# Routing as a chain of its own beside the next group's attention, for the first four groups

## The chip, the cores and the metric

The kernel runs on one core of a Trainium2 chip. The metric is the device time of one execution in microseconds; the time of a kernel is the median of its runs. The engines are TensorE (PE, with its weight loads as PEld), VectorE (DVE), ScalarE (ACT), GpSimd (POOL) and SyncE (SP, which only issues transfers here). Each takes its own instructions in order and waits on semaphores for what others make; POOL and SP also issue DMAs.

## The reference

One decoder layer over 64 sequences of 128 tokens with 256 features, all in f32: a selective-scan (Mamba) block, a retention-style attention over a context, and a mixture of experts, each followed by a layernorm of the sum with its input.

```
x = layernorm(x + mamba(x))          # layernorm, W_in, conv of 4 taps, silu, scan, gate, W_out, + x
x = layernorm(x + retention(x, ctx)) # q from x, k and v from ctx, rotated; scores * decay; @ v
x = layernorm(x + ffn(x))

# ffn, for each token t:
shared   = (silu(x Wg) * (x Wu)) Wd
probs    = sigmoid(x @ router.T + bias)          # 8 experts
w        = the two largest probs over their sum
combined = sum over the two experts e of w[t,e] * ((silu(x Wg_e) * (x Wu_e)) Wd_e)
ffn      = shared + combined
```

## The kernel before

The 64 sequences are worked off in 16 groups of four (512 tokens, `T`). A group passes through these steps, each a Python generator that issues instructions and yields:

- `front` and `scan` (together `first_half`): layernorm, W_in, convolution, gate, and the scan as products of masked matrices. They leave `acc`, in the buffer `sz`.
- `after`: W_out (`x1`, in a ring buffer of two that is also called x2), layernorm, `kh` and `v` from the context, `qh` from x1, scores, and the result `x2` with its layernorm.
- `route`: `turned` transposes x2 to `x2T`; the router's logits go through TensorE, ACT (exp) and VectorE, which ranks the experts and counts how many tokens of each expert lie before (`count`, kept from group to group); then 8 indirect DMAs (L1028), four from the row buffer of x2 and four from `row1`, a second copy, scatter the tokens' rows into `xs` in HBM, ordered by expert. ACT makes the copy row1 (L1002); VectorE adds slot and weight (L1022, L1024).
- `early_shared`: the shared expert of the group, from x2T (`shared_hidden`, `shared_down`), and a store of the sum. For the groups in `LATE` (7 to 12) it is left for the end of the kernel.
- `tile_list(k)` and `refill`: when enough groups have been routed (4, 8, 12, 16, 16), a list of expert tiles is made on VectorE, and fetches of rows and weights are issued on SP.
- `one_tile`: a tile of 256 (later 128) rows through its expert: `rows_turned`, `hidden`, `down`; results are scattered to `ys`.

The order is not written out by hand. `abreast` runs several chains of such generators together. Each chain has a position, which `placed` moves from `at` to `at + span` as its work passes, and `abreast` always advances the chain with the lowest position that isn't pausing. A yielded number is a pause, in microseconds of the planned TensorE work counted in `work`. `until` holds a chain in place until a flag is set in `states`. The chains of the first stage are:

- `first_halves` (and `second_start` for group 1): first_half(g), placed from g - 1 to g
- `second_halves`: for each group `second_half`, that is `after`, a pause, `route` and, where due, `tile_list` and `refill`, placed from g + 1 to g + 2
- `shared_ones`: early_shared(g) when the group is routed and is not in LATE
- `tiles_beside`: 57 of the 78 tiles

So in one chain the attention of group g + 1 begins after the routing of group g has ended. The instructions issued in this order then go through a scheduler that fixes the order on each engine and puts in the waits. A later instruction may be moved ahead of one that isn't ready by the scheduler's own reckoning; on the chip an engine never passes an instruction by.

Buffers carry waits too. In the pool `one` each tag has one buffer, and `qh` (of `after`) and `row1` (of `route`) share the tag "qh": a qh or a row1 can only be written when the scatters out of the last row1 have landed and the last qh has been read. `pm` has five PSUM banks, for nearly everything outside the experts, `gu` three, for gate and up products. `mhalf` and `pow` on POOL are part of every layernorm (`rstd`, L588), and so every layernorm passes through the queue in which the scatters stand.

After the first stage (`second_halves` and the rest have ended) a second `abreast` does the other 21 tiles, and a third the late shared experts and the final sums.

Of the kernel before, what the change touches and what calls it, by code (L numbers as in the profile page):

```python
# [41 lines left out]
NT = sum(n for _, _, n, _ in BATCHES)  # L42
DX = D + 2
MOST = max(n for _, _, n, _ in BATCHES)
LATE = range(7, 13)


# [455 lines left out]
def shared_decay(K):  # L503

    with ExitStack() as ctx:
        _shared_decay(ctx, K)


def _shared_decay(ctx, K):
# [114 lines left out]
    def load_x(g):  # L627
        xt = xts[g % 3]
        nc.gpsimd.dma_start(out=xt, in_=x[g * GB : (g + 1) * GB].rearrange("b l d -> l b d"))
        return xt  # L630
# [315 lines left out]
    def route(g, st):  # L946
# [79 lines left out]
        for k in range(2):  # L1026
# [6 lines left out]
            yield 5.0  # L1033
        if g in LATE:
            nc.sync.dma_start(out=x2_rows[g].rearrange("p (b d) -> p b d", d=D), in_=x2)
# [33 lines left out]
    def early_shared(g, st):  # L1069
        hid = yield from shared_hidden(st["x2T"], ring, 4)  # L1070
        yield 1.7
        for _ in shared_down(st["x2"], hid, st["x2"], gu):
            yield
        nc.sync.dma_start(out=x2_rows[g].rearrange("p (b d) -> p b d", d=D), in_=st["x2"])
# [21 lines left out]
    def tile_list(k):  # L1096
# [41 lines left out]
        nc.vector.tensor_tensor(skip[:, 0 : NE - 1], d[0:1, 1:NE], skip[:, 0 : NE - 1], ALU.add)  # L1138
        ge = small.tile([1, MOST, NE], F32, name="ge", bufs=1)[:, 0:n, :]
        nc.vector.tensor_tensor(  # L1140
# [6 lines left out]
        nc.vector.tensor_tensor(ge, ge, skip.unsqueeze(1).to_broadcast([1, n, NE]), ALU.mult)  # L1147
        row = small.tile([1, MOST], F32, name="row", bufs=1)[:, 0:n]
        nc.vector.tensor_reduce(row, ge, AX.X, ALU.add)
# [30 lines left out]
    def refill():  # L1180

        for part in range(2):
            while fetched[part] < min(room[part], known[0]):
                (fetch_down if part else fetch)(fetched[part])
                fetched[part] += 1
# [98 lines left out]
    def one_tile():  # L1284

        i = listed[0]
        listed[0] += 1
        refill()
        yield max(0.0, there[i] - work[0])
        made = yield from hidden(i)  # L1290
        room[0] = i + 1 + NW
        refill()
        if waiting:
            yield from down(*waiting.pop())
        waiting.append((i, *made))
        room[1] = i + NW
        refill()
        yield
# [13 lines left out]
    def abreast(*chains):  # L1312

        alive = [[gen, whole, 0.0, 0.0] for gen, whole in chains]
        while any(c[1] for c in alive):
            able = [c for c in alive if c[3] <= work[0]]
            if not able:
                work[0] = min(c[3] for c in alive)  # L1320
                continue
            c = min(able, key=lambda c: c[2])
            try:
                c[2], wait = next(c[0])
            except StopIteration:
                alive.remove(c)
                continue
            c[3] = work[0] + wait

    def placed(gen, at, length, span=1.0):  # L1330

        passed = 0.0
        while True:
            before = work[0]
            try:
                wait = next(gen) or 0.0
            except StopIteration:
                return
            passed += work[0] - before + wait
            yield at + span * min(1.0, passed / length), wait  # L1340

    def first_half(st):
        yield from front(st)
        yield from scan(st)

    def second_half(g, st):
        yield from after(g, st)
        yield 2.6
        yield from route(g, st)
        for k, (groups, *_) in enumerate(BATCHES):  # L1350
            if groups == g + 1:
                tile_list(k)
                refill()


    states = [{} for _ in range(NG)]
# [139 lines left out]
    def until(ready, at):  # L1496
        while not ready():
            yield at, 0.5

    def first_halves():  # L1500
        states[2]["xt"] = load_x(2)
        yield from placed(start, 0.0, 54.0)
        states[0]["scanned"] = True
        for g in range(2, NG):
            if g + 1 < NG:
                yield from until(lambda: "read" in states[g - 2], g - 1)
                states[g + 1]["xt"] = load_x(g + 1)
            yield from placed(first_half(states[g]), g - 1, 54.0)
            states[g]["scanned"] = True

    def second_start():
        yield from placed(first_half(states[1]), 0.2, 54.0)
        states[1]["scanned"] = True

    def second_halves():
        for g in range(NG):
            yield from until(lambda: "scanned" in states[g] and (g < 2 or "added" in states[g - 2]), g + 1)
            yield from placed(second_half(g, states[g]), g + 1, 60.0)
            states[g]["routed"] = True
            if g in LATE:  # L1520
                states[g]["added"] = True

    def shared_ones():

        for g in range(NG - 1):
            if g not in LATE:
                at, length = (g + 2.55, 0.45) if g + 2 in [groups for groups, *_ in BATCHES[1:]] else (g + 2, 1.0)
                yield from until(lambda: "routed" in states[g], at)
                yield from placed(early_shared(g, states[g]), at, 23.0, length)
                states[g]["added"] = True  # L1530

    def tiles_beside():

        for at, length in places:
            if at >= NG + 1:
                return
            i = listed[0]
            while i == known[0]:
                yield at, 1.0
            yield from placed(one_tile(), at, 11.0, length)  # L1540

    abreast((first_halves(), True), (second_start(), True), (second_halves(), True), (shared_ones(), True), (tiles_beside(), True))
    chains.close()


# [2 lines left out]
    def late_shared(g, last):  # L1548


        if not loaded:
            load_late(g)
            yield 4.0
        x2, x2T = loaded.pop()
        if not last:
            load_late(g + 1)
        made = shared_hidden(x2T, late, 6)
        for c in range(CF):
            yield next(made)
            if c == 1:  # L1560
                y = load_products(g)
                if unsummed:
                    yield from summed(*unsummed.pop())
        try:
            next(made)
        except StopIteration as end:
            hid = end.value
        unsummed.append((g, x2, y, hid))
        if last:
            yield 1.7  # L1570
            yield from summed(*unsummed.pop())
# [33 lines left out]
    )  # L1605
    early = [g for g in range(NG) if g not in LATE]

# [4 lines left out]
    def all_shared():  # L1612
        for i, g in enumerate(LATE):
            yield from placed(late_shared(g, g == LATE[-1]), i / len(LATE), 25.0, 1 / len(LATE))

# [221 lines left out]
```

## Time and profile before

| what | us |
|---|---|
| time, median of 3 runs | 1934.27 (1934.08 to 1934.54) |
| profiled execution, its own time | 1935.52 |
| its span in the trace | 1933.7 |
| TensorE busy | 1866.0 (97%) |
| VectorE busy | 971.9 (50%) |
| ScalarE busy | 748.7 (39%) |
| GpSimd busy | 473.1 (24%) |
| mean granted TensorE clock | 0.988 |

A matrix product in f32 shows in the trace as two matmuls and two weight loads. Matmul ends are modelled, so that the busy time of TensorE holds overlaps of neighbours; an idle time before an instruction is given in square brackets in a timeline, with what ended it. A view of busy time by stretches gives for each engine the busy time and, in brackets, the instructions; the clock is the mean of the granted TensorE clock over the stretch. A view of waits lists: engine, tile and line, what it waited for, then the time in all, how often, and the longest. Line numbers are those of the kernel before.

The first routing's logits go through TensorE at 124 us, and the scatters of the four groups' routings begin at 148.4, 214.6, 287.1 and 359.9 us.

### The profile page before, as it was taken

Reading aid. Unit: us, or ns where it says so; the run is one execution under the profiler, and the core shown is the slowest. Engines: PE = TensorE matmul, PEld = TensorE weight load, DVE = VectorE, ACT = ScalarE, POOL = GpSimd, SP = SyncE. Lnnn points to the kernel's source line nnn. Section 1 sums busy time; section 2 is a strip of 40 time slices with the busy share of each in tenths; the row PEclk is TensorE's granted clock in tenths of the full one; section 3 lists DMA queues with packets and bytes.
Section 4 is the critical chain, followed back from the end, with each engine's and each line's share of the span. In section 5 each row is a group of like instructions: output and inputs, shape, how many; then the busy total and the mean of one; then the engine's idle time right before and its main releaser. Section 6 shows DMA issues by size and latency. Waiting matters only on the chain.

```text
span 1933.7 us, 26599 instructions
## 1 busy us (share of the span) xinstructions
PE 1866.0 (97%) x9252; PEld 1393.1 (72%) x9252; DVE 971.9 (50%) x2409; ACT 748.7 (39%) x1238; POOL 473.1 (24%) x715
## 2 busy tenths in 40 slices
PE   7799999999999998999999999999999999999997
PEld 3656656668686856787877768786877888999554
DVE  5766667745455557455555474554333111111774
ACT  5553553443434343535353544352231222222233
POOL 2102212303030403132322313141313322222111
PEclk9999999999999998999999999999999999999998
DMA  4211211423150214323242224232204443353782
GB/s 142 53 35 44 68 49 41 137 85 95 45 153 28 85 35 153 101 77 113 64 133 93 79 93 123 61 123 92 81 19 128 146 150 118 120 175 107 276 305 89
DMA packets 101352, 199.10 MB, mean 103 GB/s; under 512 B 22904, under 2 KB 61432, under 8 KB 96600
## 3 DMA queue, kind: packets, MB, share of 16 engines
q1 hardware_dynamic: 80952, 144.24, 23.6%
q0 software_dynamic: 17328, 51.41, 7.8%
q10 hardware_dynamic: 2928, 1.65, 0.3%
q8 instruction: 75, 1.23, 0.3%
q14 instruction: 69, 0.57, 0.1%
HBM read 206.81 MB, written 58.08 MB: 137 GB/s over the span
## 4 chain that ended last, share of the span: by engine, by line
PE 72%; DVE 3%; issue 3%; DMA 2%; ACT 2%; POOL 2%; SPq 0%; POOLq 0%; ACTq 0%; DVEq 0%
PE pm L545 37%; PE gu L545 32%; PE pm L549 4%; DMA picked<-ys 1%; POOL rstd L588 1%; DMA ys<-rows_out,to 1%; DVE st L583 0%; DVE x L1305 0%; DMA cq<-chunks 0%; POOL xs L1028 0%; ACT x L593 0%; ACT xn L593 0%; DVE hc L1051 0%; DVE xt L1305 0%; ACT xc L667 0%
## 5 line engine op out<-in xcount | busy, mean ns | idle before, releaser
L545 PE MATMUL gu<-rows_T,routed_gu 128*128 128x256 f32 (+1 forms) x2496 | 499.4, 351 | 1.5 <-ACT rows_T L1232 1.5
L545 PEld LDWEIGHTS gu<-rows_T,routed_gu 128*128 128x128 f32 x2496 | 417.7, 191 | 59.2 <-issue 14.2
L1261 DVE TENSOR_TENSOR hid<-hid,gu 128x512 f32<-128x512 f32 x135 | 92.7, 687 | 394.8 <-PE gu L545 344.4
L545 PE MATMUL pm<-routed_d,hid 128*128 128x256 f32 x1080 | 252.7, 381 | 0.0
L545 PE MATMUL gu<-x2T,shared_w 128*128 128x512 f32 x512 | 232.0, 596 | 4.4 <-DVE hc L1051 3.3
L545 PE MATMUL pm<-xnT,w_in_s 128*128 128x512 f32 x480 | 226.6, 599 | 1.7 <-ACT xnT L606 1.1
L545 PEld LDWEIGHTS pm<-routed_d,hid 128*128 128x128 f32 x1080 | 199.7, 190 | 29.6 <-issue 5.4
L1277 POOL DMA_INDIRECT ys<-rows_out,to x135 | 135.0, 1000 | 331.4 <-ACT rows_out L1276 282.8
L545 PEld LDWEIGHTS gu<-x2T,shared_w 128*128 128x128 f32 x512 | 94.3, 190 | 112.1 <-issue 93.6
L593 ACT ACTIVATE x<-x,shift,rstd 128x256 f32<-128x256 f32 x156 | 82.3, 590 | 232.5 <-DVE shift L590 222.2
L588 POOL TENSOR_TENSOR rstd<-var,mhalf 128x4 f32<-128x4 f32 (+1 forms) x69 | 72.8, 1055 | 370.6 <-DVE var L586 318.6
L662 DVE SCALAR_TENSOR_TENSOR xc<-pm,cw,xc 128x508 f32<-128x508 f32 (+1 forms) x180 | 131.4, 738 | 37.2 <-ACT xc L657 36.0
L545 PEld LDWEIGHTS pm<-xnT,w_in_s 128*128 128x128 f32 x480 | 90.2, 192 | 80.3 <-issue 72.3
L1276 ACT ACTIVATE rows_out<-pm,wt 128x256 f32<-128x256 f32 x135 | 57.9, 471 | 205.2 <-PE pm L545 185.4
L1260 ACT ACTIVATE hid<-gu 128x512 f32<-128x512 f32 x135 | 80.6, 597 | 110.0 <-PE gu L545 109.7
L545 PE MATMUL pm<-w_out_s,sz 128*128 128x256 f32 x512 | 116.4, 381 | 0.4 <-ACT xd L807 0.2
L545 PEld LDWEIGHTS pm<-w_out_s,sz 128*128 128x128 f32 x512 | 95.4, 191 | 14.3 <-issue 1.0
L657 ACT ACTIVATE xc<-pm,cb,cw 128x512 f32<-128x512 f32 x60 | 46.7, 778 | 144.2 <-PE pm L545 144.2
L1028 POOL DMA_INDIRECT xs<-x,index x64 | 71.6, 1118 | 78.0 <-DVE row L1024 42.8
L583 DVE BATCH_NORM_STATS2 st<-x 128x6 f32<-128x256 f32 x196 | 77.4, 408 | 1.6 <-DMA x<-in_x_dram 0.7
L545 PE MATMUL gu<-shared_w,hc 128*128 128x256 f32 x320 | 72.5, 380 | 0.0
L1051 DVE TENSOR_TENSOR hc<-hc,gu 128x512 f32<-128x512 f32 x64 | 43.5, 680 | 55.2 <-PE gu L545 35.1
(288 smaller groups left out, 2571.2 us busy)
## 6 DMA issues: line engine op xcount, KB each, us to landing
routed_gu<-in_ffn_dram SPq DMA_DIRECT2D x78, 1024.0 KB
routed_d<-in_ffn_dram SPq DMA_DIRECT2D x78, 512.0 KB
picked<-ys SPq DMA_DIRECT2D x16, 1024.0 KB
rows_in<-xs SPq DMA_DIRECT2D x57, 258.0 KB
cT<-in_ctxT_dram POOLq DMA_DIRECT2D x16, 512.0 KB, 4.1
x_rows<-x SPq DMA_DIRECT2D x16, 512.0 KB
cq<-chunks SPq DMA_DIRECT2D x15, 512.0 KB
x<-in_x_dram POOLq DMA_DIRECT2D x9, 512.0 KB, 4.2
```

The costliest lines, as they stand in the source:

```text
L545: nc.tensor.matmul(out, lhsT=lhsT, rhs=rhs, **how)
L549: nc.tensor.transpose(out, src, ident)
L583: nc.vector.bn_stats(st, src[:, b, :])
L588: nc.gpsimd.tensor_tensor(rstd, var, mhalf[:, 0:n], ALU.pow)
L593: nc.scalar.activation(dst[:, b, :], src[:, b, :], AF.Identity, bias=shift[:, b : b + 1], scale=rstd[:, b : b + 1])
L657: nc.scalar.activation(xcf[:, c, :], ps, AF.Identity, bias=cb[:, c : c + 1], scale=cw[:, c, TAPS - 1 : TAPS],)
L662: nc.vector.scalar_tensor_tensor(xc[:, c, :, s:], ps3[:, :, : L - s], cw[:, c, TAPS - 1 - s : TAPS - s], xc[:, c, :, s:], ALU.mult, ALU.add,)
L1028: s = nc.gpsimd.indirect_dma_start(out=xs, in_=rows[k][:, b, :], in_offset=None, out_offset=bass.IndirectOffsetOnAxis(ap=index[:, b, k : k ...
L1260: nc.scalar.activation(hc, psg, AF.Silu)
L1261: nc.vector.tensor_tensor(hc, hc, psu, ALU.mult)
L1276: nc.scalar.activation(y[:, j, :], ps[:, j, :], AF.Copy, scale=wt[:, j : j + 1])
L1277: s = nc.gpsimd.indirect_dma_start(out=ys, in_=y[:, j, :], in_offset=None, out_offset=bass.IndirectOffsetOnAxis(ap=to[:, j : j + 1], axis=0),)
```

## The change

For the groups 0 to 3 (`APART`) the chain `second_halves` now runs only `after`, placed from g + 1 to g + 1.6, and goes on to the attention of the next group. A new chain, `routings`, waits until x2 of the group is there, pauses 2.6 as the old chain did, and runs `routing` (the rest of the old second_half: `route`, `tile_list`, `refill`) placed from g + 1.6 to g + 2. Group 4 and later ones are issued as before; `second_halves` holds there until the group before is routed. The instructions are the same ones; what `abreast` issues, and the scheduler orders, is their interleaving.

```diff
+APART = range(0, 4)
 ...
     def second_half(g, st):
         yield from after(g, st)
         yield 2.6
+        yield from routing(g, st)
+
+    def routing(g, st):
         yield from route(g, st)
         for k, (groups, *_) in enumerate(BATCHES):
             if groups == g + 1:
                 tile_list(k)
                 refill()
 ...
     def second_halves():
         for g in range(NG):
             yield from until(lambda: "scanned" in states[g] and (g < 2 or "added" in states[g - 2]), g + 1)
+            if g in APART:
+                yield from placed(after(g, states[g]), g + 1, 38.0, 0.6)
+                continue
+            yield from until(lambda: g == 0 or "routed" in states[g - 1], g + 1)
             yield from placed(second_half(g, states[g]), g + 1, 60.0)
             states[g]["routed"] = True
             if g in LATE:
                 states[g]["added"] = True
+
+    def routings():
+
+        for g in APART:
+            yield from until(lambda: "x2" in states[g], g + 1.6)
+            yield g + 1.6, 2.6
+            yield from placed(routing(g, states[g]), g + 1.6, 26.0, 0.4)
+            states[g]["routed"] = True
 ...
-    abreast((first_halves(), True), (second_start(), True), (second_halves(), True), (shared_ones(), True), (tiles_beside(), True))
+    abreast((first_halves(), True), (second_start(), True), (second_halves(), True), (routings(), True), (shared_ones(), True), (tiles_beside(), True))
```

## The prediction

> **What bounds the kernel now.** I read the page's busy rows and slices first, then the busy time by stage, then TensorE's waits, then GpSimd's timeline.
>
> ```profile
> span 1933.7 us, 26599 instructions
> PE 1866.0 (97%) x9252; PEld 1393.1 (72%) x9252; DVE 971.9 (50%) x2409; ACT 748.7 (39%) x1238; POOL 473.1 (24%) x715
> PE   7799999999999998999999999999999999999997
> PEclk9999999999999998999999999999999999999998
> ```
>
> TensorE is the bound: the span less its busy time is 67.7 us, and the change removes no work. It can win only idle time and time at a reduced clock. Here a rule speaks for much more. The Trainium skill ("Perfetto Trace Analysis", section Identifying the Most-Contended Engine) says that matmul busy share is no measure of headroom and that the weight loads' busy share is: 72%, or 28% of 1933.7 = 540 us left. Those 540 us are no time that an order of chains can fill: 400 to 720 us shows loads 230.1 of 320 us and no idle matmul time at all. I use the waits; by the rule a gain of tens of microseconds would be within reach.
>
> ```profile
> core 0: us, PE busy (x) PEld busy (x) DVE busy (x) ACT busy (x) POOL busy (x), PEclk, DMA share, GB/s
> 93.00:145.00 52.00, 45.76 (x205) 25.79 (x204) 35.21 (x78) 27.27 (x41) 5.68 (x5) 0.93 0.12 33
> 145.00:218.00 73.00, 71.61 (x348) 47.37 (x347) 47.25 (x129) 35.27 (x54) 19.13 (x17) 0.98 0.18 55
> 218.00:290.00 72.00, 69.47 (x335) 44.89 (x335) 48.84 (x122) 34.14 (x53) 15.74 (x16) 1.00 0.18 53
> 290.00:355.00 65.00, 62.45 (x277) 40.33 (x276) 43.05 (x108) 29.43 (x47) 11.15 (x12) 1.00 0.15 47
> 355.00:400.00 45.00, 41.17 (x208) 28.15 (x207) 33.45 (x88) 17.82 (x28) 16.58 (x24) 0.96 0.54 191
> 400.00:720.00 320.00, 320.00 (x1553) 230.10 (x1553) 170.92 (x407) 130.57 (x210) 68.79 (x79) 1.00 0.23 70
> 720.00:748.00 28.00, 20.77 (x128) 18.02 (x125) 20.90 (x74) 9.45 (x14) 11.59 (x10) 0.76 0.31 99
> ```
>
> ```profile
> PE pm L549 <- ACT xn L593: 8.7, 9, 2.0
> PE pm L545 <- DVE sel L985: 2.8, 1, 2.8
> ```
>
> Each stretch: length, then busy time of each engine, then clock. From 93 us (where routing begins to matter) to 400, where group 3's routing has been turned into expert tiles, TensorE idles 6.2 + 1.4 + 2.5 + 2.6 + 3.8 = 16.5 us, and the clock costs at most 52 x 0.07 + 73 x 0.02 + 45 x 0.04 = 6.9 us. So the four routings that move lie in a region with only 23 us to win. The second view's two rows are its longest waits from 90 to 400 us (in all, times, longest): most are the transposes of a later group's normalized x, one is routing's own (sel). Another pocket is 720 to 748 us (7.2 us idle, 28 x 0.24 = 6.7 us of clock), when group 7's routing runs and the fillers have run out.
>
> ```profile
> 148.43 1.11 POOL L1028 DMA_INDIRECT xs<-x,index  x1 [14.29 <-ACT xd L807]
> 149.84 0.99 POOL L1028 DMA_INDIRECT xs<-x,index  x1 [0.30 <-DVE xc L817]
> 158.01 0.96 POOL L1028 DMA_INDIRECT xs<-row,index  x1 [0.30 <-issue]
> 378.77 0.19 POOL L1234 CAST to<-rows_in 128x2 int32<-128x2 f32 x1 [3.10 <-DMA rows_in<-xs]
> 379.04 1.05 POOL L588 TENSOR_TENSOR rstd<-var,mhalf 128x4 f32<-128x4 f32 x1
> ```
>
> A routing ends in eight scatters on GpSimd's queue: from 148.43 to 158.97 is 10.5 us, and the view of that line has 2.6 us (median) from issue to landing, so the eighth lands some 13 us after its row is written. The last two rows are a queue effect: a layernorm's rstd stands behind the first tile's `to`, which waits for fetched rows.
>
> **The change, part by part.** No instruction is added or removed but a few ACT table loads (929 against 917 in the program's order; 12 x 1.28 us on an engine 39% busy, hidden by its slack). What moves is the order on all engines, from TensorE's first changed row, after the last W_in product of group 2 at 120.6 us, to the end of the stage before the remaining tiles; the last 4,466 of TensorE's 5,998 rows are unchanged.
>
> Removed. (a) 93 to 145: the 2.0 us wait (xn) and 0.6 us (sc) precede the first changed row and stay, and so does the clock lost before 103 (93 to 103 us ran at 0.83, 1.7 us). W_out of group 1 (32 matmuls of 256 columns; sixteen of 512 took 7.03 us at 113.6, so 7 us) now stands at 120.6, so 3.6 us of idle go, and with the wait for sel the clock of 138 to 150 us (0.72 there, 12 x 0.28 = 3.4 us): 7.0. (b) The 1.4 us in 145 to 218. (c) 355 to 400: in the new order the two layernorms' rstd stand ahead of `to`, and after(4) begins sooner: most of 3.8 + 1.8 = 5.6. (d) 720 to 748: each attention now runs about one group nearer to its own first half, so group 9's first half is still there to fill group 7's routing. The trace of before can't show how well; between 0 and all 13.9 I take 5. Sum 19.0.
>
> Added, from the new order and this trace's durations (VectorE 128x512 0.6 to 0.7 us, 128x1024 1.2, a layernorm's statistics 2.4, pow 1.0, its four ACT rows 2.1):
> (e) Group 1's attention and group 2's scan now share VectorE with routing(0). From 130 to 159 us VectorE works nearly through; TensorE waits 0.9 us for x1T and 0.6 for qh: 1.5.
> (f) Next stand x2T of group 1, the third shared chunk and xn of group 3. Scatter 1 of routing(0) is ahead of rstd on POOL: 1.8 us. `hc` is behind 4.7 us of scan rows on VectorE and frees the gu bank late: 1.8 us. Then a new wait: ACT's copy of row1 for group 1 must wait until routing(0)'s last scatters have landed, since row1 has one buffer (tag qh). In before the copy came at 193.9, more than 30 us after the landings. Scatters begin at about 163, share POOL with the pow and land at 176.5; behind that copy on ACT stand hc and the four xn rows, and on VectorE row1's own update and shift. The first transpose of xn can start at 178.8, TensorE is there at 174.3: 4.5 us. Together 8.1.
> (g) The same buffer again: qh of group 3 is now written after row1 of group 2, and waits for its four landings. Counting from group 2's x2T transposes: row1 ends at 18.2, scatters 18.4 to 29.0, landed 31.4; TensorE has W_V, W_in, W_Q until 30.3, then lacks a pm bank (the convolution's taps stand behind qh on VectorE) until 32.7 and waits for qh's second half until 36.4: 2.4 + 2.0 = 4.4. In before group 2's qh came at 244.1, 15 us after the last landing.
> (h) Waits of 2 us and more have cost clock: 1.7 us after that for xn at 93, 3.4 us after that for sel. For (f) and (g) I take 2.0 + 1.7 = 3.7; bounds 0 and 7.
> (i) routing(3) runs beside scan(4) and shared(2) alone, since second_halves waits for it: like (e) but with less to fill: 3, bounds 0 and 7.
> Costed at nothing: SP's queue keeps its instructions, and the x2_rows stores move with shared_ones (VectorE waits for them 3 times, 9.9 us in all, before as after). cT on POOL can go once the qh of the group before has been multiplied, 20 us ahead of its own product (landing 4.1 us); load_x stands behind the scatters as before. If that cover went, each would cost its 4 us landing at most.
> Sum 1.5 + 8.1 + 4.4 + 3.7 + 3.0 = 20.7, so +1.7 net. Bounds of (e) to (g): below by half, should ACT and VectorE run ahead of my reading; above by as much again.
>
> A rule that speaks against the change: the Trainium skill ("SBUF — State Buffer", section A bandwidth-pool intuition that's wrong) says that a DMA issued from GpSimd waits for its descriptors while a VectorE copy holds the shared port, about 620 ns alone against 3,100 ns. The trace has scatters of 0.96 us mostly and up to 1.88 us beside work. In the new order they run beside attention. By the rule, eight take 25 us rather than 10.5, and (f) and (g) grow by 14 us each; by the rows, if all were at 1.88 + 0.30, by 7 each. Most VectorE rows here are not copies: I stay with 10.5.
>
> **How it stands to the runs.** The profiled execution took 1935.52 us (span 1933.7, 1.8 around it), 1.25 above the median of 1934.27. 1935.5 + 1.7 = 1937.2 by its own time, 1936.0 against the median.
>
> **The rivals.**
> 1. Trade, as summed (chance 0.39): -4 to +8, so 1930 to 1942.
> 2. Slower: the one buffer of row1 and qh decides. If all scatters stretch to 1.88 us (+7 at (f) and at (g)) it is 1936 + 14 = 1950; with two thirds of that 1946, my figure for it. For: the order of ACT and VectorE, in-order queues. Against: short scatters when VectorE is light. It decides (over 0.2% slower) once both landings come 1.1 us later than counted: 1.7 + 2.2 = 3.9. 0.30.
> 3. Faster: the new waits are filled, since matmuls of shared stand ready, and more of (d) comes: -19 - 6 (of the rest of (d)) + 14 = -11, 1923. For: VectorE is busy 74% at most in these stretches. Against: TensorE's order is fixed, so a wait isn't jumped over. 0.28.
> 4. It does next to nothing, because abreast interleaves by position and TensorE's order hardly moves. Against: 1,000 of its rows differ. 0.03.
>
> Removing all 23 us up to 400 would bound the gain there: a forecast beyond 1934 - 23 - 14 = 1897 has no ground.
>
> **How the numbers follow.** About 0.2% (3.9 us) is what a measurement of this kernel can tell from no change. Case 1 spreads as 0.02 faster, 0.24 within, 0.13 slower; with case 3, case 4 and case 2 that makes faster 0.30, same 0.27, slower 0.43. The range 1922 to 1950 leaves out half of case 3's lower tail (0.11) and case 2's upper end (0.09). Case 1 alone: 1930 to 1942.
>
> **What would show it.** In the profile after: no wait of TensorE for sel near 141 us, and a clock above 0.93 there; waits of TensorE for xn near 175 to 180 us, put down to ACT and behind it a row1 copy that waits for a scatter; VectorE's qh once waiting for a DMA, 4 us of TensorE idle after; rstd ahead of `to`; 20.8 busy of 28 us bettered where group 7 is routed. Wrong if TensorE's idle time up to group 3's tiles falls by more than 6 us (then 3), if it rises by more than 8 (then 2), or if the difference arises after 400 us in a place that none of these names.

## The result and the profile after

The changed kernel took 1947.83 us (median of 4 runs, 1945.1 to 1950.58) against 1934.4 us of the kernel before (4 runs, 1934.08 to 1936.76): ratio 1.006, interval 1.0047 to 1.0073. It is slower, by 13 us. The profiled execution took 1948.26 us, its span was 1946.6 us, its mean clock 0.986. Line numbers of the changed kernel that appear here are 1 higher than before (in e2 and e9, 5 higher from `route`'s row1 on).

The page's busy rows and slices of the changed kernel:

```profile
span 1946.6 us, 26642 instructions
PE 1869.5 (96%) x9252; PEld 1394.3 (72%) x9252; DVE 987.9 (51%) x2409; ACT 764.6 (39%) x1250; POOL 468.0 (24%) x715
PE   6898999999999989999999999999999999999997
PEclk9899999999999999999999999999999999999998
```

The span less TensorE's busy time is now 77.1 us (67.7 before), and the mean clock fell from 0.988 to 0.986. Nearly all the loss is idle time and reduced clock of TensorE; the work is the same. Where it lies is read from the same stretches as before (length, then busy time and instructions of each engine, clock, DMA):

```profile
core 0: us, PE busy (x) PEld busy (x) DVE busy (x) ACT busy (x) POOL busy (x), PEclk, DMA share, GB/s
93.00:145.00 52.00, 48.61 (x222) 30.70 (x220) 35.94 (x91) 26.07 (x43) 7.53 (x7) 1.00 0.17 43
145.00:218.00 73.00, 65.64 (x319) 42.76 (x318) 46.30 (x124) 33.24 (x48) 22.48 (x22) 0.95 0.19 56
...
355.00:400.00 45.00, 44.95 (x217) 30.06 (x216) 24.32 (x61) 23.18 (x33) 6.35 (x11) 1.00 0.42 138
400.00:720.00 320.00, 312.75 (x1552) 229.63 (x1551) 185.74 (x448) 129.50 (x209) 71.61 (x83) 0.99 0.23 73
720.00:748.00 28.00, 28.00 (x93) 16.35 (x93) 18.39 (x33) 13.17 (x19) 5.79 (x13) 1.00 0.56 184
...
820.00:1270.00 450.00, 436.73 (x2252) 335.69 (x2251) 248.66 (x606) 203.69 (x329) 114.38 (x157) 0.98 0.29 90
```

The last stretch, in the kernel before:

```profile
820.00:1270.00 450.00, 446.95 (x2317) 345.60 (x2316) 249.05 (x618) 197.60 (x325) 125.11 (x170) 1.00 0.30 94
```

From 93 to 145 us the idle time falls from 6.2 to 3.4 us and the clock is whole; from 355 to 400 us hardly any idle time is left. From 145 to 218 us it rises from 1.4 to 7.4. Over 93 to 400 us, idle time and half clock together fall from 23.4 us (16.5 + 6.8) to 18.7 (13.6 + 5.1). Behind group 3, where routing is issued in one chain as before, 820 to 1270 us was full and is full no longer: 13.3 us of idle time instead of 3.1, with a lower clock.

The pocket at 720 us looks filled, but it has moved. Group 7's routing (its sel product) stands at 706.5 us instead of 726.7, and most of the 7.3 us of idle time in 400 to 720 us is there (columns as above):

```profile
686.00:714.00 28.00, 22.93 (x166) 19.13 (x165) 21.47 (x54) 13.47 (x21) 4.15 (x4) 0.88 0.23 74
```

That is 5.1 us of idle time and 3.4 of clock, where the pocket of before had 7.2 and 6.7. So it costs some 5 us less than before, and isn't gone.

Since work moves between stretches, I also set the two traces side by side at equal work: the time at which TensorE had begun the same amount of matmul work, reckoned from the sizes and starts of its rows. The work is given as microseconds at full clock. After less before:

| work done | 140 | 180 | 260 | 380 | 700 | 740 | 820 | 1260 | 1380 to the end of the tiles |
|---|---|---|---|---|---|---|---|---|---|
| us | -5.7 | +3.3 | +6.7 | -7.7 | +6.1 | -7.7 | -2.6 | +15.9 | +12.5 |

The entries depend on what a row is reckoned to cost, and the traces show that only roughly for small products: with other costs for these most entries move by 1 to 3 us, and that at 700 by up to 8, since it lies between the pocket of after, which is past by then, and that of before, which is not. So the 13.8 us lost from 380 to 700 and won back from 700 to 740 are largely the moved pocket. What is left is plain: up to the end of group 3's routing the change gains 8 us (5 by idle time and clock), from 380 to 740 the table has nothing won or lost on balance, and between 820 and 1260 it loses 18.5 us.

TensorE's waits in the changed kernel, first 90 to 400 us, then 400 to 1480 us (in all, times, longest):

```profile
PE pm L550 <- ACT xn L594: 7.9, 2, 5.9
PE pm L546 <- DVE xc L663: 2.0, 1, 2.0
PE pm L550 <- ACT x L594: 1.4, 2, 1.2
PE pm L546 <- ACT x1T L605: 0.8, 1, 0.8
PE pm L546 <- DVE sc L899: 0.6, 1, 0.6
PE pm L546 <- DVE pre L992: 0.5, 1, 0.5
```

```profile
PE pm L546 <- DVE cj L782: 13.3, 6, 4.1
PE pm L546 <- DVE mk L1005: 4.4, 1, 4.4
PE pm L546 <- DVE d L758: 1.7, 1, 1.7
```

The row for cj has grown: before it was 2.3 us in one wait. cj is an operand of the scan (`scan`, pm<-cj,bj), and is VectorE's product of cj with `eb`, an exponential that ScalarE makes. Parts of the timeline of all engines around the fourth of the six waits:

```profile
863.29 1.08 PE L546 MATMUL pm<-middle,dlb 128*32 128x128 f32 x32
...
863.52 1.01 POOL L1278 DMA_INDIRECT ys<-rows_out,to  x1 [0.30 <-issue]
864.54 1.06 POOL L589 TENSOR_TENSOR rstd<-var,mhalf 128x4 f32<-128x4 f32 x1
...
865.84 0.60 ACT L594 ACTIVATE x<-x,shift,rstd 128x256 f32<-128x256 f32 x1 [5.47 <-DVE shift L591]
...
866.81 1.59 ACT L594 ACTIVATE x<-x,shift,rstd 128x256 f32<-128x256 f32 x3
...
868.77 1.04 ACT L1003 COPY row<-x 128x1028 f32<-128x1028 f32 x1
869.83 1.28 ACT L779 ACT_TABLE_LOAD   x1
...
871.13 0.69 ACT L779 ACTIVATE eb<-pm,a_col 128x512 f32<-128x512 f32 x1
...
872.46 0.68 DVE L782 TENSOR_TENSOR cj<-cj,eb 128x512 f32<-128x512 f32 x1
...
873.29 2.05 PE L546 MATMUL pm<-cj,bj 128*128 128x128 f32 x8 [4.07 <-DVE cj L782]
```

What eb reads (pm<-middle,dlb) is there at 864.4. But ScalarE's next instruction is not eb: it is the first of the four x rows, the last layernorm of an attention, and ScalarE stands idle 5.47 us for it, because rstd, whose input var is there at 859.8, stands on GpSimd behind the scan's own product for cj (860.64) and two scatters of a tile. Then come the other x rows, the row1 copy of that group's routing, and a table load, so eb starts at 871.13, 6.8 us after its input was there. TensorE runs out of work and waits 4.07 us, and the trace has it at half clock for 6.8 us from 871.3 on, which costs another 3.4. The source line of eb in the two kernels over 400 to 1480 us, after and then before:

```profile
L779 ACT ACTIVATE eb<-pm,a_col x10: 687/687/688, 498.8 to 1356.9; 128x512 f32<-128x512 f32 x10
its engine sat idle before it (us, times) until:
  PE pm L546: 2.0, 1
who waited for it (us, times):
  DVE bj L781: 12.6, 9
```

```profile
L778 ACT ACTIVATE eb<-pm,a_col x10: 670/687/688, 441.4 to 1277.3; 128x512 f32<-128x512 f32 x10
its engine sat idle before it (us, times) until:
  PE pm L545: 20.3, 8
who waited for it (us, times):
```

Before, ScalarE sat waiting for eb's input in 8 of 10 cases and nobody waited for eb. After, its input waited for ScalarE in 9 of 10, and VectorE waited for eb 9 times. From the start of the last pm<-middle,dlb matmul to that of eb the ten cases sum to 5.7 us before and 41.7 after. The program's order shows the same: for the groups 5 to 15, ScalarE's list has x rows or the row1 copy of another group within four entries ahead of eb ten times after, and never before. I call this the meeting: the end of one group's attention meets the scan of a later one on ScalarE.

It has a second place. A group later VectorE, too, stands idle for the rstd of that layernorm, with the scan's d right behind, and TensorE then waits 1.7 us for d:

```profile
963.43 1.23 DVE L591 SCALAR_TENSOR_TENSOR shift<-mv,rstd 128x4 f32<-128x4 f32 x1 [5.33 <-POOL rstd L589]
...
964.82 0.19 DVE L758 TENSOR_TENSOR d<-dl,place 128x64 f32<-128x64 f32 x1
```

### The profile page after: what moved, and what is told of

The parts are those of the page before. It is cut to its first block, busy times and chain, and to the rows that moved or that the text cites. A ratio compares the mean times of both kernels' runs of the same rounds, so it can differ in the third digit from the quotient of the medians.

```text
span 1946.6 us, 26642 instructions
## 1 busy us (share of the span) xinstructions
PE 1869.5 (96%) x9252; PEld 1394.3 (72%) x9252; DVE 987.9 (51%) x2409; ACT 764.6 (39%) x1250; POOL 468.0 (24%) x715
## 4 chain that ended last, share of the span: by engine, by line
PE 76%; DVE 4%; issue 3%; DMA 3%; ACT 3%; POOL 2%; SPq 0%; ACTq 0%; POOLq 0%; DVEq 0%
PE pm L546 41%; PE gu L546 31%; PE pm L550 4%; POOL rstd L589 1%; DMA picked<-ys 1%; DVE st L584 1%; ACT x L594 1%; DMA bj<-rows 0%; DMA ys<-rows_out,to 0%; ACT L779 0%; DVE x L1306 0%; DVE hc L1052 0%; ACT row L1003 0%; DMA rows_in<-xs 0%; DMA xs<-row,index 0%
## 5 line engine op out<-in xcount | busy, mean ns | idle before, releaser
L1029 POOL DMA_INDIRECT xs<-x,index x64 | 65.2, 1019 | 132.6 <-issue 35.6
L1052 DVE TENSOR_TENSOR hc<-hc,gu 128x512 f32<-128x512 f32 x64 | 43.6, 682 | 65.8 <-PE gu L546 54.3
L1233 ACT COPY rows_T<-pm 128x512 f32<-128x512 f32 (+1 forms) x78 | 41.0, 526 | 91.1 <-PE pm L550 91.1
```

Source lines behind the costliest of these rows:

```text
L1029: s = nc.gpsimd.indirect_dma_start(out=xs, in_=rows[k][:, b, :], in_offset=None, out_offset=bass.IndirectOffsetOnAxis(ap=index[:, b, k : k ...
```

## The experiments

Theories. The meeting, as above. The lost lead: since attention ran ahead for four groups, the first halves stay about a group behind for good, and this as such costs. The shared buffer: row1 and qh, rival 2. Chance: any order other than the one before has waits of its own of such a size. The runs were made in three sets of four, on three chips; the kernel before took 1947.92, 1936.23 and 1947.25 us in them (medians), so only ratios within a set are compared. The recorded expectations count eb without group 1, where it has another name: from 4 on, their group numbers for eb are one too low.

| run | edit | set | us | ratio to before, interval |
|---|---|---|---|---|
| e1_lead | after, attention held for the next first half | 1 | 1975.02 | 1.014 (1.0123 to 1.0157) |
| e2_row1 | after, row1 in its own buffer | 1 | 1961.55 | 1.008 (1.0056 to 1.0104) |
| e3_before_lag | before, first halves held, pause 6 | 1 | 1945.02 | 0.9993 (0.9983 to 1.0003) |
| e4_apart3 | after, groups 0 to 2 apart | 1 | 1951.14 | 1.0017 (1.0008 to 1.0025) |
| c_before | before, unchanged | 2 | 1937.91 | 1.0002 (0.9993 to 1.0012) |
| c_after | after, unchanged | 2 | 1946.6 | 1.0048 (1.0034 to 1.0062) |
| e5_after_lag | after, first halves held, pause 6 | 2 | 1933.79 | 0.9991 (0.9983 to 1.0) |
| e6_shift8 | after, a pause of 8 for 1.1 in the attention | 2 | 1938.0 | 1.001 (1.0003 to 1.0016) |
| e7_meet | before, first halves held, pause 2 | 3 | 1944.62 | 0.9988 (0.998 to 0.9995) |
| e7_nomeet | before, first halves held, pause 10 | 3 | 1948.25 | 1.0002 (0.9993 to 1.0011) |
| e8_apart1 | after, group 0 alone apart | 3 | 1947.02 | 0.9997 (0.9989 to 1.0006) |
| e9_lag_row1 | e5 with e2's buffers | 3 | 1943.43 | 0.998 (0.9973 to 0.9987) |

**Giving the lead back (e1).** From group 4 on, the attention waits for the first half of the next group.

```diff
-            yield from until(lambda: g == 0 or "routed" in states[g - 1], g + 1)
+            yield from until(lambda: "routed" in states[g - 1] and (g + 1 == NG or "scanned" in states[g + 1]), g + 1)
```

> The changed kernel, but from group 4 on the attention of a group waits until the first half of the next group has ended, as it did by itself in the kernel before. Theory of the lead (the four routings apart let attention catch up with the first halves, and the waits after 800 us come from the lost lead): the gain of 8 us that stands at the end of group 3's tiles stays and the loss after 820 us goes, so 1926, between 1922 and 1932; TensorE's waits for cj fall from 13.3 us to under 5. Theory of the shared buffer (row1 and qh): nothing before 400 us changes, so it stays at 1946 to 1949.

It became slower still. The hold stretched one group: group 4's routing comes 154 us after group 3's, in the changed kernel 89. Meanwhile the chain of tiles went on, and the tiles ran out: the trace has no gate or up product of a tile from 572.7 to 785.7 us (before: 656.4 to 764.8), and at equal work the kernel loses 9 us between 700 and 740, where group 7 is routed, and 12 between 860 and 1260. No wait put down to cj is left, as expected, but others took their place (400 to 1480 us):

```profile
PE pm L546 <- ACT x1T L605: 11.5, 4, 4.7
PE pm L546 <- DVE d L758: 6.3, 1, 6.3
```

So both forecasts missed. The run shows that what a hold displaces can cost more than what it repairs; it neither supports nor excludes the lost lead.

**A buffer for row1 (e2).** The weight buffers are empty until the first tiles.

```diff
-        rows = [st["row"], one.tile([P, GB, DX], F32, name="row1", tag="qh")]
+        if g < 3:
+            row1 = weights[(2, 0, 1)[g]][0][:, 0 : GB * DX].rearrange("p (b d) -> p b d", d=DX)
+        else:
+            row1 = one.tile([P, GB, DX], F32, name="row1", tag="qh")
+        rows = [st["row"], row1]
```

> The changed kernel, but row1 of the groups 0, 1 and 2 lies in parts of the expert weight buffers, which are free then, and not in the buffer of qh. Theory of the shared buffer: the 5.9 us wait for xn, the 2.0 us wait for pm after xc and the half clock behind them (6.8 and 3.4 us long, 5.1 us of work) go, 13 us in all, so 1935. Theory of the lead: these waits go too, but since the trace places the loss after 820 us, which stays, the time ends between 1935 and 1941 and the excess of after over before between 820 and 1260 us of equal work (about 16 us) is unchanged; if the waits before 400 us return elsewhere it stays at 1946.

The wait after xc at 284 us went entirely and the wait for xn fell to 3.8 us; at 380 of equal work it stood 3 us better than the changed kernel. Its ratio (1.008) is no better, though the changed kernel was not run in this set: the loss between 820 and 1260 is there (24 us), with waits for cj of 10.9 us. TensorE's order differs from that of the changed kernel in four places, all before group 3's attention, yet this trace also has 12.7 us of waits for xnT, which the changed kernel doesn't have in its own traces on other chips. Those I can't explain; they make the buffer's share of the total time unreadable here. That the buffer is the cause of the loss is excluded by where the loss lies.

**The lag alone (e3).** In the kernel before:

```diff
+            if g > 5:
+                yield from until(lambda: "x2" in states[g - 2], g - 1)
+                yield g - 1, 6.0
             yield from placed(first_half(states[g]), g - 1, 54.0)
```

> The kernel before with its routing in one chain, but from group 6 on a first half starts only when x2 of two groups earlier has been made, plus a pause of 6 us of planned work, so that its lead over attention is about as small as in the changed kernel. Theory of the lead: slower than before by 8 to 20 us, 1942 to 1954, with waits of TensorE for cj of over 8 us in all after 800 us. Theory of the shared buffer, or of the moved routings themselves: no more than 3 us from before, 1931 to 1937.

No difference. From group 9 on the first halves are as late against attention as in the changed kernel: the first W_in product of group 11 starts 73 us ahead of group 10's first kh product in the kernel before, 12 us ahead in the changed kernel, and here 3 us behind it. But eb stands behind x or row1 in two groups only (10 and 11). So the theory of the lost lead falls: being a group closer costs nothing in itself.

**Three groups apart (e4).**

```diff
-APART = range(0, 4)
+APART = range(0, 3)
```

> The changed kernel with routing apart for groups 0 to 2 only. In the order that the chains then take, the first halves keep 0.8 of the lead that they have before (0.2 with groups 0 to 3). Theory of the lead: most of the loss after 820 us is gone and most of the gain before 400 us stays, 1926 to 1934. Theory that each routing moved apart costs its share: three quarters of 13 us, 1944; theory of the shared buffer: its two waits are in groups 1 and 3, so 1940 to 1948.

1.0017, a third of the loss of four; eb stands behind x in one group only (5). The loss doesn't go by how many routings are moved. In this trace TensorE's longest wait after 400 us is 4.9 us for d, in the pocket of group 7's routing, and the cj waits are 3.9 us. Yet eb is late here as well, 31.4 us in ten cases, mostly behind rows of an expert tile (hid, rows_out) that wait for TensorE. So a late eb doesn't always make TensorE wait: its three waits for cj after 400 us are 0.8 to 1.6 us here.

**Controls (c_before, c_after).**

> The kernel before, unchanged, for its time and profile on the chip of these runs. Every theory: it is its own yardstick, ratio 1; where its profile shows more idle time than the first one, the added waits belong to the chip and are taken off the others.

> The changed kernel, unchanged, beside the others. Every theory: ratio to before 1.005 to 1.008, and again waits of TensorE for cj of about 13 us after 400 us, because they come from the order of ScalarE's instructions (eb stands behind the four x rows and the row1 copy in nine of the groups 4 to 14, in the kernel before in none).

Both came as expected. c_after has cj waits of 14.8 us (8 times), a delay of eb of 40.8 us in the same ten cases, and at equal work loses 19.0 us between 820 and 1260 against c_before. The loss belongs to the order, not to a chip.

**Moving the meeting, two ways (e5, e6).** e5 puts e3's edit into the changed kernel. e6 changes one number, in `after` ahead of the product with v:

```diff
         nc.vector.tensor_tensor(sc, pss, dec.unsqueeze(1).to_broadcast([P, GB, L]), ALU.mult)
-        yield 1.1
+        yield 1.1 if g < 4 else 8.0
```

> The changed kernel with the hold of the first halves that was tried on the kernel before: from group 6 on a first half starts only after x2 of two groups earlier and a pause of 6. In ScalarE's order eb then stands behind x and the row1 copy in one group only (4). Theory of the meeting (scan's eb on ScalarE behind the end of the attention): the loss after 820 us goes and the gain of the first 400 us stays, so 0.3 to 0.7% below the changed kernel and at or below before, ratio 0.995 to 1.001, waits for cj under 5 us. Theory of the lost lead: no lead is given back, so ratio 1.005 to 1.010. Theory that any other order than that of before, which is tuned, has its own chance waits of this size: 1.003 to 1.010, with the waits elsewhere.

> The changed kernel, with the pause ahead of the attention's last product (after sc) lengthened from 1.1 to 8 us of planned work for the groups from 4 on, so that the end of the attention comes later against the scan; nothing else. In ScalarE's order eb stands behind the four x rows and the copy in none of the groups 4 to 14, and behind one x row set in one. Theory of the meeting: waits for cj under 5 us, ratio 0.995 to 1.002. Theory of the lost lead: 1.005 or more, since attention still starts with the first half of the next group hardly begun. Theory of chance waits: 1.003 to 1.010, with the waits elsewhere.

Both came as the meeting expects. e6 has no wait for cj of 0.2 us or more after 400 us, its eb is delayed 9.3 us in ten cases, and its stretch 820 to 1270 is full again at full clock:

```profile
820.00:1270.00 450.00, 447.29 (x2334) 347.31 (x2333) 256.52 (x611) 205.53 (x328) 129.97 (x169) 1.00 0.31 94
```

At equal work e6 loses 2.3 us between 820 and 1260 and e5 gains 2.8, where c_after lost 19.0 (all against c_before). So 7 us of planned pause in one place take 0.4% off the time, with no work, buffer or engine changed. But the pause moves more than the meeting: 4,612 of TensorE's 9,252 rows in the trace have another place in its order and, against the expectation, the lead doesn't stay small. The first W_in product of group 11 starts 64 us ahead of group 10's first kh product again (changed kernel 12, before 73). So e6 can't tell the meeting from the lost lead. e5 can: there that W_in product starts 12 us behind kh, the lead is smaller than in the changed kernel, and the loss is gone all the same. What both versions have in common is that eb stands free. The theory of chance falls with these runs too: e3, e5 and e6 are three other orders, and all lie within 0.1% of before. Both versions still gain 9 us up to 380 of equal work and lose it by the end of the pocket: e5 has 14.0 us of idle time from 690 to 735 us.

```profile
690.00:735.00 45.00, 31.03 (x199) 24.71 (x197) 28.45 (x96) 14.57 (x27) 14.17 (x19) 0.81 0.33 99
```

**Making the meeting in the kernel before (e7).** e3's edit with a pause of 2 and, in the second kernel, of 10:

```diff
                 yield from until(lambda: "x2" in states[g - 2], g - 1)
-                yield g - 1, 6.0
+                yield g - 1, 2.0
```

> The kernel before, routing in one chain, with the hold of the first halves from group 6 on, but with a pause of 2 instead of 6. In ScalarE's order eb then stands behind the x rows or the row1 copy in six of the groups 4 to 14 (5 and 10 to 14), in four of them with the copy. Theory of the meeting: waits of TensorE for cj of 4 to 8 us after 900 us, and a time 4 to 10 us above that of the same kernel with a pause of 10, where eb stands behind them in no group; ratio to before 1.001 to 1.005. Theory of the lost lead: both pauses alike. Theory of the moved routings: both at 1.000.

> The same with a pause of 10: the lead of the first halves is no larger than with 2, and eb stands behind the end of the attention in no group. Theory of the meeting: ratio 0.997 to 1.001, waits for cj under 3 us. Theory of the lost lead: 1.003 or more.

This missed in the total, where the version with the meetings is 0.14% the faster one, and in TensorE's waits for cj, which are 1.5 us in e7_meet and not 4 to 8. The source line of eb, with the pause of 2 and of 10, shows that the meeting was made, at half the size of the changed kernel's:

```profile
  DVE bj L780: 5.5, 5
```

```profile
  DVE bj L780: 1.9, 2
```

Between 860 and 1260 of equal work e7_meet loses 20.5 us and e7_nomeet 13.1 against c_before, which is on another chip (e8 below, with the order of before on e7's own chip, loses 3.7 there). The difference of the two, 7.4, is as forecast, and it can be found among the waits: from 860 to 1300 us TensorE waits 8.4 us for x2T, d, cj and dlb in e7_meet and not at all for them in e7_nomeet. What else e7_nomeet loses there is no meeting. And e7_meet stood 5.7 us better at 860, since its pocket at group 7 was filled (-8.3 against -0.8 at 740), and it was spared 5.2 us that e7_nomeet lost at 1460, where the next run shows a loss of the chip's own. So meetings do cost, yet where the pauses fall in the pocket weighs as much, and the place of eb in the order does not by itself foretell the time of a kernel.

**Group 0 apart (e8).**

```diff
-APART = range(0, 4)
+APART = range(0, 1)
```

> The changed kernel with routing apart for group 0 only (range(0, 1)). From group 2 on the chains then take the same positions as in the kernel before, and eb stands behind the end of the attention in no group. Theory of the meeting: step (a) of the prediction comes alone, 6 us at 140 us of equal work, without the waits of (f) and (g), and stays to the end: ratio 0.996 to 0.998. If (f) comes with the first routing already, or the gain is given back where the filler runs out at 720 us: 0.999 to 1.001.

The edit changes no order: group 1 is no longer in `APART`, so its attention waits until group 0 is routed, and every instruction of TensorE, VectorE, ScalarE and GpSimd stands where it stood in the kernel before. So the expectation, that step (a) would come alone, is not tested. As a repeat of the kernel before it gives the size of what a chip does: against c_before its trace is 7.9 us later at the end of the first stage, of which 4.7 lie in one place (1460 of equal work), with waits for which the profile names no releaser (3.0 us, "issue").

**Lag and buffer (e9).** The edits of e3 (pause 6) and e2 together, in the changed kernel.

> The changed kernel with the hold of the first halves and a pause of 6, and with row1 of the groups 0 to 2 in the weight buffers, so without the single buffer's waits. If (f) and (g) are the buffer's cost and stay gained: 2 to 5 us below the same without the row1 edit, which was at 0.9991, so 0.9965 to 0.998. If they are given back in the pocket at 720 us, where the gain of 4 us was lost with the hold alone: 0.999.

0.998, the fastest of all and faster than both kernels, by 3.8 us against before (e7_meet is 0.1% faster than before too). At 260 and 380 of equal work it is 2.3 and 2.2 us better than e5 (against c_before, other chip). The wait for xn is still 3.8 us, although no buffer holds row1 up any longer, and the trace of it shows why:

```profile
172.88 0.97 POOL L1033 DMA_INDIRECT xs<-routed_gu,index  x1 [0.30 <-issue]
173.88 1.04 POOL L589 TENSOR_TENSOR rstd<-var,mhalf 128x4 f32<-128x4 f32 x1
174.96 0.16 DVE L591 SCALAR_TENSOR_TENSOR shift<-mv,rstd 128x4 f32<-128x4 f32 x1 [4.36 <-POOL rstd L589]
175.16 2.08 ACT L594 ACTIVATE xn<-x,shift,rstd 128x256 f32<-128x256 f32 x4 [4.25 <-DVE shift L591]
175.81 1.18 PE L550 MATMUL pm<-ident,xn 128*128 128x128 f32 x4 [3.82 <-ACT xn L594]
```

group 3's rstd stands behind the last scatters of group 0's routing on GpSimd.

## Why the prediction was right and wrong

The outcome that it held likeliest (slower, 0.43) came, and 1947.8 is inside its range, but 12 us above its figure and outside its likeliest case. That it fell inside the range owes something to luck, because two errors have opposite signs. From 93 to 400 us idle time and half clock fell by 4.7 us, where the steps sum to 14.0 gained and 20.7 lost. Behind that, some 18 us were lost where 5 of gain had been taken. The figure of rival 2, 1946, is nearly the measured one, for a cause that isn't it.

- (a), 7.0 gained: right. No wait for sel is left near 141 us, and the clock from 138 to 150 us is 1.00 instead of 0.72. That the clock is whole from 93 us on is not the change's doing: the half-clock window at 96.4 us, ahead of the first changed row, is gone, and one at 65.8 us is as much longer.
- (c), 5.6 gained: 355 to 400 us has 0.05 us of idle time and full clock, though it holds other work now, since routing(3)'s sel stands at 329.5 us instead of 353.1. (b), 1.4: not to be told from (f), whose waits fall into the same stretch.
- (e), 1.5 lost: 0.8, for x1T. None came for qh.
- (f), 8.1 lost: the size nearly right (1.2 for x, 5.9 for xn; no gu bank was late). The mechanism stands in the trace of the changed kernel: ScalarE's row1 copy waits for the scatters, and the xn rows stand behind it.

```profile
176.38 1.05 ACT L1003 COPY row<-x 128x1028 f32<-128x1028 f32 x1 [7.24 <-DMA xs<-row,index]
177.34 0.59 ACT L1051 ACTIVATE hc<-gu 128x512 f32<-128x512 f32 x1
177.83 2.06 ACT L594 ACTIVATE xn<-x,shift,rstd 128x256 f32<-128x256 f32 x4
```

The share of the buffer in (f) was mis-sized: with a buffer of its own the wait for xn is still 3.8 us in both runs (e2, e9), so the buffer is worth about 2 and GpSimd's queue the rest. The prediction had counted only scatter 1 ahead of an rstd.

- (g), 4.4 lost: 2.0 measured for xc and 0.3 for qh; in e2 and e9 neither is left. (i), 3.0: 0.5.
- (h), 3.7: half-clock windows of 6.8 and 3.4 us behind the waits for xn and pm cost 5.1. Its ground, that waits of 2 us and more cost clock, is not safe: the wait of 2.0 us for xn at 95 us has no such window behind it in the changed kernel, where in the kernel before the same wait, at 93 us, had one.
- The steps that lose, (e) to (i), sum to 20.7, and the waits and windows named here to 16 us: (g) and (i) above all were over-sized.
- The scatters beside VectorE's work: median 0.97 us, at most 1.89 us in the changed kernel (row of their source line), so the rows were the right measure. No scatter here took the some 3 us that the rule of the Trainium skill ("SBUF — State Buffer", section A bandwidth-pool intuition that's wrong) would have made of each.
- The 540 us of headroom by the other rule (weight loads at 72%) didn't show: the load share is 72% after too, and the best of all orders tried won 3.8 us.
- How far the order changes was misread. The prediction has the last 4,466 of TensorE's 5,998 rows unchanged; in the traces only the last 2,262 of 9,252 are, from 1459 us on. Everything from 120.6 to 1459 us could move. Nor are the table loads always hidden by ScalarE's slack: where eb is late, as at 871 us, one of 1.28 us stands between the row1 copy and eb.
- (d) is the step that failed: "each attention now runs about one group nearer to its own first half", from which it took 5 us of gain. The nearness came, and the pocket did get cheaper by some 5 us, though it was moved and not filled. What the step left out is what else the nearness does for the ten groups to come. It moves the end of every attention, four x rows that wait for GpSimd and a copy, to just before the scan's eb on ScalarE. That costs 18.5 us between 820 and 1260: waits for cj, d, dlb and x2T of 12.6 us there (9.6 of them for cj), where all waits of before were 2.9, and half-clock windows of 17.0 us in all, which take 8.5 us. The prediction costed the change up to 400 us in detail and what lies behind with one term that could only be a gain; its own last sentence named this way to be wrong.

Open: why the same order of instructions takes 11 us more on one chip than on another, how the waits in the pocket at 700 to 740 us could be foretold from an order, and how much a meeting costs in another order: in e7 it cost 7 us in its stretch, and the total didn't show it.

## What to carry to other kernels

When chains are planned together by position, a change to the first few rounds sets the phase of all later ones: read which instruction of one chain each in-order engine holds just ahead of the other chain's, for a late round too, and not only where the edit is. An instruction that waits for a slow queue (here a layernorm's x rows for GpSimd's pow behind scatters) is cheap until something urgent stands behind it on the same engine. The cure may be one pause: test it by moving the phase, before rebuilding buffers, and look in the trace at what the pause moved, which may be far more than its own length (e6).

## What was not expected of the hardware

- The kernel before, with every instruction in the same place, took medians of 1934.4, 1947.92, 1936.23 and 1947.25 us in the four sets of runs: up to 0.7%, as much as the effect under study. The ratio of the change, taken twice within a set, held (1.006 and 1.0048).
- Waits of about 4 us cost almost as much again in clock: in the changed kernel half-clock windows of 6.8 us, 3.4 us of work each, stand at the waits of 4.1 us at 869 and 1251 us. The waits of 0.9 to 1.5 us for cj at 500, 601, 773 and 1154 us had none. In between it varies: a wait of 1.7 us for d at 963 us had one of 3.4 us, that of 2.0 us for xn at 95 us none.
